# A graph layer whose row gathers are shared out: SyncE fetches one unit in 45 row by row, and the packing of edges is rewritten

## The chip, the core and the metric

The kernel runs on one core of one Trainium2 chip. A core has five engines, each with its own stream of instructions that it works off in order: PE (TensorE, matrix products), DVE (VectorE, elementwise work and sums), ACT (ScalarE), POOL (GpSimd) and SP (SyncE, which only issues transfers and waits). SP, ACT and POOL can issue DMA transfers; each has a queue of its own. The engines wait for each other by semaphores. SBUF is the on-chip memory of 128 partitions, PSUM the accumulator memory that PE writes, and DRAM holds inputs and outputs. The metric is the time of one execution on the device in microseconds (us), less is better.

## The reference

A message-passing layer on a graph with 50,000 nodes of 160 numbers and 1,650,000 edges, sorted by destination node (`dst`), followed by a residual and a layer norm. 50,000 of the edges are self loops (source = destination).

```python
s, v = x[:, :64], x[:, 64:].reshape(n, 32, 3)
ss, vv = s[src], v[src]                      # one row of x for each edge
e0, e1 = sh[:, 0:1], sh[:, 1:4]              # four numbers of each edge
dot = einsum('eui,ei->eu', vv, e1)
out0 = C0 * (ss * e0 @ W1 + dot * INV3 @ W2)
p3 = (ss @ W3)[:, :, None] * e1[:, None, :] * INV3
p4 = einsum('eui,uw->ewi', vv * e0[:, :, None], W4) * INV3
p5 = einsum('eui,uw->ewi', cross(vv, e1[:, None, :]), W5) * INV6
m = concatenate([out0, (C1 * (p3 + p4 + p5)).reshape(-1, 96)], axis=1)
m_agg = segment_sum(m, dst, num_segments=n)  # sum over the edges of each node
h = concatenate([m_agg[:, :64] @ Ws * LIN_S,
                 einsum('nui,uw->nwi', m_agg[:, 64:].reshape(n, 32, 3), Wv) * LIN_V ...])
return layernorm(x + (x + relu(h)))
```

What is computed is linear in `x[src]` for each of the four edge numbers, so the sums over edges can be taken before the weights.

## The kernel before

**Units, groups, pairs.** A unit is 128 edges, a group is 6 units (768 edges), a pair is two groups (12 units); 2100 groups make 12,600 units and 1050 pairs. The destinations of one group lie in a window of W = 32 nodes. For each unit POOL issues one indirect transfer (`gather`, L288), which fetches the 128 rows of x named by `si` into `xg`. DVE builds `hot` (L297: edge against slot in the window) and `ha` (L300: times the four edge numbers), and PE multiplies `ha` by the fetched rows into `ps` (L325), six units to a group. DVE or ACT takes `ps` to `A` (L334, L330). Four groups form a chunk: PE transposes it (L436), ACT copies it out (`at`, L439), PE applies the weights (L450), ACT copies the result to `hp` (L454). For each block of 128 nodes PE gathers the chunks that touch it (L480), and DVE and ACT add the residual and normalise (L176 to L192).

**Packing.** Self loops need no fetch from afar: their rows lie one after the other from the window's first node. Groups 100 to 2079 are made of L = 787 edges each, of which K = 19 self loops are taken out, so that 768 remain. `pack` does this for 120 groups at once, one to a partition, as a generator whose pieces are emitted between the pairs. It loads the edges (L351 to L354), casts them (L356), marks self loops (L370) and counts them (L371), then sums each of the four edge numbers of the self loops for each of the 32 slots (L389: one instruction for each of two halves of the row, four numbers and 32 slots, 256 in all), and closes the gaps with masked shifts (L406 to L416). The result goes to DRAM (`sd`, `ad`, L422, L423) and comes back with `load` (L241, L242). `own` fetches the 32 rows of each group's window, four copies, into `xo` (L315, the address comes from a register that L310 loads), and L334 adds `xo` times the self loops' sums (`taken`) to the group's sum.

**Order.** The work is emitted pair by pair in the loop of L595, with `own` three pairs ahead; a scheduler then orders each engine's stream and inserts the semaphore waits. SP issues nearly all transfers that are not gathers, ACT only the weights and the stores of the result (L192). The pools set how far an engine can be ahead: `rows` has six buffers of 12 units for `xg`, `own` four for `xo`, `psA` two for `ps`.

**Helpers, not in use.** The code already has a way to fetch a unit row by row with an ordinary queue (`fetch`, L505): 32 row offsets at a time are loaded into registers, and each row is one transfer. The table that says which engine does so, and every how many units, is empty:

```python
HELP = {}
...
for h, (eng, period) in enumerate(HELP.items()):
```

Of the kernel before, what the change touches and what calls it, by code (L numbers as in the profile page):

```python
# [34 lines left out]
F32 = mybir.dt.float32  # L35
# [9 lines left out]
P = 128  # L45
MUL0, MUL1 = 64, 32
D = MUL0 + 3 * MUL1
NK = 4
# [14 lines left out]
HELP = {}  # L63
HEAD = 100
RP = 120
ROWS = 32
# [28 lines left out]
def tile_gnn_resnorm(ctx: ExitStack, tc: tile.TileContext, x, src, dst, attr, W1, W2, W3, W4, W5, Ws, Wv, out, n_edges):  # L95
# [92 lines left out]
    def norm3(pool, y, mv, rstd, n, row):  # L188
        nc.vector.reciprocal(rstd[:n], rstd[:n])  # L189
        o = pool.tile([P, D], F32, name="o")  # L190
        nc.vector.tensor_scalar(o[:n], y[:n], mv[:n, 0:1], rstd[:n], op0=ALU.subtract, op1=ALU.mult)  # L191
        nc.scalar.dma_start(out[row, :], o[:n])  # L192
# [18 lines left out]
    with tc.tile_pool(name="once", bufs=1) as once, tc.tile_pool(name="raw", bufs=2) as rawp, \  # L211
            tc.tile_pool(name="idx", bufs=2) as idxp, tc.tile_pool(name="rows", bufs=6) as rowp, \
            tc.tile_pool(name="far", bufs=3) as farp, tc.tile_pool(name="own", bufs=4) as ownp, \
# [13 lines left out]

        offsets = {}
        evict = nc.vector.tensor_copy if ET.Activation in HELP else nc.scalar.copy

        def load(s):
# [4 lines left out]
            if NH <= g0 < NH + NPK:  # L236
# [3 lines left out]
                for i in range(2):  # L240
                    nc.sync.dma_start(rf[:n, i, :], sd[i:i + 1, e].rearrange("o (u p) -> (o u) p", p=P))  # L241
                nc.sync.dma_start(ra[:n].rearrange("u p k -> u (p k)"), ad[e].rearrange("(u p) k -> u (p k)", p=P))  # L242
# [3 lines left out]
            nc.sync.dma_start(ri[:n, 0, :], src1[e].rearrange("(u p) o -> u (p o)", p=P))  # L246
            nc.sync.dma_start(ri[:n, 1, :], dst1[e].rearrange("(u p) o -> u (p o)", p=P))
            nc.sync.dma_start(ra[:n].rearrange("u p k -> u (p k)"), attr[e].rearrange("(u p) k -> u (p k)", p=P))
# [55 lines left out]

        def own(p):

            s, g, ng = pairs[p]
            if not NH <= g < NH + NPK:
                return
            _, at = nc.values_load_multi_w_load_instructions(  # L310
                baseO[0:1, g:g + ng], engines=[ET.SP], min_val=0, max_val=(N - W) * 4 * D,
                skip_runtime_bounds_check_because="an offset of a row of x")
            xo = ownp.tile([P, PG, D], F32, name="xo")
            for i, v in enumerate(at):
                nc.sync.dma_start(xo[:, i, :].bitcast(U8),  # L315
                                  xbytes[ds(v, W * 4 * D)].rearrange("(w f) -> w f", w=W).unsqueeze(0)
                                  .to_broadcast([NK, W, 4 * D]))
# [20 lines left out]
        owns, stored, taken = {}, {}, {}  # L338
        halves = ((0, L // 2), (L // 2, L))

        def pack(c):
# [9 lines left out]
            nc.sync.dma_start(pri[:n, 0, :], src1[e].rearrange("(r e) o -> r (e o)", e=L))  # L351
            nc.sync.dma_start(pri[:n, 1, :], dst1[e].rearrange("(r e) o -> r (e o)", e=L))
# [468 lines left out]
```

## Time and profile before

| what | us |
|---|---|
| median of three runs | 18,925.2 (18,899.5 to 18,944.2) |
| the profiled execution | 15,879.8 |
| its span | 15,878.0 |
| busy: PE / POOL / DVE / ACT | 11,902 / 11,926 / 7,961 / 898 |
| transfers: bytes moved | 1382 MB, 87 GB/s |
| granted PE clock | 0.648 of full |

The profile is of one execution, and that one was shorter than the timed runs by a factor of 1.19. Busy time does not count the issuing of transfers by SP and ACT, nor the time between two instructions. The page cuts the span into 40 slices; the digits are tenths of busy time:

```profile
DVE  4565555545454554545454554545455454545422
...
POOL 7677777777777777777777777777777777777776
```

In groups of instructions, the columns are line, engine, operation, tiles and count, then the busy time in us and the mean of one in ns, then the engine's idle time ahead of the group and what ended it:

```profile
L389 DVE SCALAR_TENSOR_TENSOR waste<-marks,pra 120x393 bf16<-120x393 f32 (+3 forms) x4352 | 3652.5, 839 | 2.9
```

### The profile page before, as it was taken

To read this page: it belongs to the slowest core of one execution; us is meant where nothing else is said; L and a number is where in the kernel's file an instruction comes from. 1 tells how busy PE (TensorE), PEld (TensorE's weight loads), DVE (VectorE), ACT (ScalarE), POOL (GpSimd) and SP (SyncE) were. 2 spreads that over 40 slices of the span, in tenths; PEclk is the share of its full clock that TensorE was granted. 3 is DMA by queue.
4 is the path that set the end of the run, shared out by engine and by line. 5 is a ranking of instruction groups with operands and counts; after the bars stand their busy time and mean duration, and the time that the engine had idled before them with its cause. 6 is when DMAs were issued, how large, how long until landed. Compare 5 with 4: busy or idle time off the path is not lost. (4 is left out here: it accounts for less than half of the span.)

```text
span 15878.0 us, 132047 instructions
## 1 busy us (share of the span) xinstructions
PE 11902.0 (75%) x43059; PEld 8781.1 (55%) x43060; DVE 7960.7 (50%) x17460; ACT 897.9 (6%) x2069; POOL 11926.1 (75%) x12611
## 2 busy tenths in 40 slices
PE   7677777777777777777777777777777777777777
PEld 4455555555555555555555555555555555555555
DVE  4565555545454554545454554545455454545422
ACT  0000000000000000000000000000000000000000
POOL 7677777777777777777777777777777777777776
PEclk7666666666666666666666666666666666666666
DMA  3333333333333333333333333333333333333332
GB/s 83 74 86 94 84 82 96 82 95 84 94 83 92 85 82 96 83 96 83 94 85 87 91 82 96 84 94 84 94 83 82 96 82 96 83 93 84 86 83 70
DMA packets 1040422, 1382.05 MB, mean 87 GB/s; under 512 B 233153, under 2 KB 813393, under 8 KB 1035641
## 3 DMA queue, kind: packets, MB, share of 16 engines
q0 software_dynamic: 604800, 1033.00, 26.9%
q1 hardware_dynamic: 378065, 307.98, 7.1%
q10 hardware_dynamic: 56864, 32.58, 0.7%
q8 instruction: 344, 5.64, 0.1%
q14 instruction: 349, 2.86, 0.1%
HBM read 1303.90 MB, written 68.75 MB: 86 GB/s over the span
## 5 line engine op out<-in xcount | busy, mean ns | idle before, releaser
L288 POOL DMA_INDIRECT xg<-in_x,si x12600 | 11924.5, 946 | 3917.0 <-issue 3527.0
L325 PE MATMUL ps<-xg,ha 128*128 128x160 f32 x25200 | 8037.7, 447 | 3686.5 <-DMA xg<-in_x,si 3640.6
L325 PEld LDWEIGHTS ps<-xg,ha 128*128 128x128 f32 x25200 | 5302.5, 266 | 6227.7 <-DMA xg<-in_x,si 6033.2
L334 DVE SCALAR_TENSOR_TENSOR A<-xo,taken,ps 128x160 f32<-128x160 f32 x1980 | 728.8, 377 | 7231.3 <-PE ps L325 7231.3
L389 DVE SCALAR_TENSOR_TENSOR waste<-marks,pra 120x393 bf16<-120x393 f32 (+3 forms) x4352 | 3652.5, 839 | 2.9
L300 DVE TENSOR_TENSOR ha<-hot,pk 128x1536 f32<-128x1536 f32 x1050 | 1830.2, 1744 | 284.1 <-PE ps L325 284.0
L480 PE MATMUL phb<-hp,hot 128*128 128x160 f32 x4544 | 1181.0, 433 | 56.2 <-ACT at L439 52.8
L480 PEld LDWEIGHTS phb<-hp,hot 128*128 128x128 f32 x4544 | 1066.4, 297 | 173.3 <-ACT at L439 172.2
L436 PE MATMUL pt<-ident,A 128*128 128x128 f32 (+1 forms) x4200 | 1051.7, 406 | 100.1 <-ACT hp L454 67.8
L450 PE MATMUL phc<-BWb,at 32*128 32x160 f32 x4200 | 1078.0, 404 | 0.0
L439 ACT COPY at<-pt 128x512 f32<-128x512 f32 (+1 forms) x1050 | 596.9, 579 | 6815.1 <-PE pt L436 6746.4
L450 PEld LDWEIGHTS phc<-BWb,at 32*128 32x128 f32 x4200 | 835.0, 253 | 196.3 <-issue 196.1
L450 PE MATMUL phc<-BWa,at 128*128 128x160 f32 x4200 | 922.6, 374 | 2.3 <-ACT at L439 2.0
L436 PEld LDWEIGHTS pt<-ident,A 128*128 128x128 f32 (+1 forms) x4200 | 700.7, 178 | 302.7 <-ACT hp L454 143.1
L450 PEld LDWEIGHTS phc<-BWa,at 128*128 128x128 f32 x4200 | 847.0, 255 | 35.3 <-ACT at L439 35.3
L297 DVE TENSOR_TENSOR hot<-bank,rel 128x384 f32<-128x384 f32 x1050 | 569.6, 544 | 0.3
L454 ACT COPY hp<-phc 128x160 f32<-128x160 f32 x525 | 153.3, 292 | 6230.2 <-PE phc L450 6171.5
L470 DVE TENSOR_TENSOR hot<-bank,rr 128x768 f32<-128x768 f32 (+2 forms) x391 | 358.8, 918 | 0.1
L389 DVE DVE_READ_ACCUMULATOR waste<-marks,pra 120x1 f32 (+1 forms) x4352 | 342.9, 79 | 0.0
L416 DVE COPY_PREDICATED pra<-marks,pra 120x1572 f32<-120x1572 int32 (+6 forms) x170 | 323.5, 1903 | 0.0
L176 DVE SCALAR_TENSOR_TENSOR y<-phb,xt 128x160 f32<-128x160 f32 x391 | 120.6, 308 | 195.6 <-PE phb L480 195.3
L414 DVE COPY_PREDICATED prs<-marks,prs 120x393 f32<-120x393 int32 (+6 forms) x340 | 181.3, 582 | 0.1
(98 smaller groups left out, 1610.1 us busy)
## 6 DMA issues: line engine op xcount, KB each, us to landing
xg<-in_x,si POOLq DMA_INDIRECT x12600
xo<-in_x SPq DMA_DIRECT2D x1980, 80.0 KB
xt<-in_x SPq DMA_DIRECT2D x390, 80.0 KB
out<-o ACTq DMA_DIRECT2D x390, 80.0 KB
ra<-ad SPq DMA_DIRECT2D x99, 240.0 KB
pra<-in_attr SPq DMA_DIRECT2D x16, 1475.6 KB
ad<-pra SPq DMA_DIRECT2D x16, 1440.0 KB
rf<-sd SPq DMA_DIRECT2D x198, 60.0 KB
```

Of the source, the lines that this page charges most:

```text
L288: nc.gpsimd.indirect_dma_start(out=xg[:, j, :], out_offset=None, in_=x, in_offset=bass.IndirectOffsetOnAxis(ap=placed[0][:, u + j:u + j + ...
L297: nc.vector.tensor_tensor(hot[:, :n], slotsP[:, 0:W].unsqueeze(1).to_broadcast([P, n, W]), rel[:, u:u + n].unsqueeze(2).to_broadcast([P, n ...
L300: nc.vector.tensor_tensor(ha[:, :n], hot[:, :n].unsqueeze(2).to_broadcast([P, n, NK, W]), pk[:, :, u:u + n].rearrange("p k u -> p u k").un ...
L325: nc.tensor.matmul(ps[:, j // G, :], ha[:, j].rearrange("p k w -> p (k w)"), xr, start=j % G == 0, stop=j % G == G - 1)
L334: nc.vector.scalar_tensor_tensor(A[:, i], xo[:, i], taken[r // RP][:, r % RP:r % RP + 1], ps[:, i], op0=ALU.mult, op1=ALU.add)
L389: nc.vector.scalar_tensor_tensor(waste[:n, a:e], m[:, q], float(w + 1), pra[:n, a:e, k], op0=ALU.is_equal, op1=ALU.mult, accum_out=mine[:n ...
L416: nc.vector.copy_predicated(pra[:n, a:e], mi[:, r].unsqueeze(2).to_broadcast([n, e - a, NK]), pra[:n, a + d:e + d])
L436: nc.tensor.transpose(pt[:f1 - f0, g, :], A[:, i, f0:f1], ident)
L439: evict(at[:, :, :ng].rearrange("f k g w -> f g k w"), pt[:f1 - f0, :ng].rearrange("f g (k w) -> f g k w", w=W))
L450: nc.tensor.matmul(ph[:ng * W], at[:, k, :ng].rearrange("f g w -> f (g w)"), bw[:, k, :], start=i == 0, stop=i == 2 * NK - 1)
L470: nc.vector.tensor_tensor(hot2[:, :len(cs)], slotsP.unsqueeze(1).to_broadcast([P, len(cs), P]), rr[:, :len(cs)].unsqueeze(2).to_broadcast( ...
L480: nc.tensor.matmul(ph[:nb], hot2[:r, i, :nb], hp[:r], start=i == 0, stop=i == len(cs) - 1)
```

## The change

- `HELP` now names SP with a period of 45: of every 45 units the last of some pair is fetched by SP, 128 transfers of one row of 640 bytes, in four batches of 32 offsets (`ROWS`). POOL has 279 gathers less, 12,321. The offsets come from a copy of the source indices times 640 that ACT makes for each 20 groups (`ro`).
- All other transfers that SP issued go through ACT's queue (`dq`), `own` among them; it loads the addresses of ten groups at once (`OWN`), and `xo` has five buffers instead of four.
- The store of the result is issued one pair after its computation (`do_send`).
- In `pack` the sums for slot w run only over the part of the row where edges of that slot can lie (`early`, `late`), with two more limits that are tested at the end beside the others. That makes 168 instructions of 213 elements on average instead of 256 of 393.
- In `pack` the comparison of source and destination takes the destinations from a copy in PSUM, made by ACT; the count is capped in the scan itself, and operations from SBUF to SBUF are folded into others that have one operand in PSUM.
- Pauses (`yield`) stand between the loads and the cast of a pack, and ahead of its stores.

```diff
-HELP = {}
+HELP = {ET.SP: 45}
 HEAD = 100
 RP = 120
-ROWS = 32
+
+ROWS = {ET.SP: 32, ET.Activation: 16}
...
-                    nc.sync.dma_start(rf[:n, i, :], sd[i:i + 1, e].rearrange("o (u p) -> (o u) p", p=P))
-                nc.sync.dma_start(ra[:n].rearrange("u p k -> u (p k)"), ad[e].rearrange("(u p) k -> u (p k)", p=P))
+                    dq.dma_start(rf[:n, i, :], sd[i:i + 1, e].rearrange("o (u p) -> (o u) p", p=P))
+                dq.dma_start(ra[:n].rearrange("u p k -> u (p k)"), ad[e].rearrange("(u p) k -> u (p k)", p=P))
...
+        OWN = 5
+
         def own(p):
 
             s, g, ng = pairs[p]
             if not NH <= g < NH + NPK:
                 return
-            _, at = nc.values_load_multi_w_load_instructions(
-                baseO[0:1, g:g + ng], engines=[ET.SP], min_val=0, max_val=(N - W) * 4 * D,
-                skip_runtime_bounds_check_because="an offset of a row of x")
+            if p % OWN == 0:
+                g1 = min(g + OWN * PG, NH + NPK)
+                _, at = nc.values_load_multi_w_load_instructions(
+                    baseO[0:1, g:g1], engines=[ET.Activation], min_val=0, max_val=(N - W) * 4 * D,
+                    skip_runtime_bounds_check_because="an offset of a row of x")
+                places.update(enumerate(at, g))
             xo = ownp.tile([P, PG, D], F32, name="xo")
-            for i, v in enumerate(at):
-                nc.sync.dma_start(xo[:, i, :].bitcast(U8),
-                                  xbytes[ds(v, W * 4 * D)].rearrange("(w f) -> w f", w=W).unsqueeze(0)
-                                  .to_broadcast([NK, W, 4 * D]))
+            for i in range(ng):
+                dq.dma_start(xo[:, i, :].bitcast(U8),
+                             xbytes[ds(places.pop(g + i), W * 4 * D)].rearrange("(w f) -> w f", w=W).unsqueeze(0)
+                             .to_broadcast([NK, W, 4 * D]))
             owns[p] = xo
...
+        degree = n_edges / N
+        late = 6 * math.sqrt(L) + 2 * degree
+        early = -6 * math.sqrt(L)
...
+            for _ in range(3):
+                yield
             nc.scalar.copy(prs[:n], pri[:n])
             yield
             marks = psP.tile([P, 512], F32, name="marks")
             m, mi = marks[:n], marks[:n].bitcast(I32)
-            cum = packp.tile([P, L], F32, name="cum")
+
+            cum = packp.tile([P, L + 1], F32, name="cum")
             far = packp.tile([P, L], I32, name="far")
             less = packp.tile([P, L], I32, name="less")
-            carry = packp.tile([P, 1], F32, name="carry")
-            pbf = packp.tile([P, 1], F32, name="pbf")
+            pbf = packp.tile([P, 2], F32, name="pbf")
             mine = packp.tile([P, 2, NK * W], F32, name="mine")
             waste = packp.tile([P, L], BF16, name="waste")
-            nc.vector.tensor_scalar(pbf[:n], pb[:n], float(N - W), None, op0=ALU.min)
+            nc.vector.tensor_scalar(pbf[:n, 0:1], pb[:n], float(N - W), None, op0=ALU.min)
+            nc.vector.tensor_scalar(pbf[:n, 1:2], pbf[:n, 0:1], -1.0, None, op0=ALU.add)
+            nc.vector.memset(mine, 0.0)
+            nc.vector.memset(cum[:, 0:1], 0.0)
+
             for h, (a, e) in enumerate(halves):
                 q = slice(0, e - a)
-                nc.vector.tensor_tensor(m[:, q], prs[:n, 0, a:e], prs[:n, 1, a:e], op=ALU.is_equal)
-                nc.vector.tensor_tensor_scan(cum[:n, a:e], m[:, q], zeros[:n].to_broadcast([n, e - a]),
-                                             carry[:n] if h else 0.0, op0=ALU.add, op1=ALU.add)
-                nc.vector.tensor_copy(carry[:n], cum[:n, e - 1:e])
+                col = slice(2 * c + h, 2 * c + h + 1)
+                nc.scalar.copy(m[:, q], prs[:n, 1, a:e])
+                nc.vector.tensor_tensor(m[:, q], prs[:n, 0, a:e], m[:, q], op=ALU.is_equal)
+                nc.vector.tensor_tensor_scan(cum[:n, a + 1:e + 1], m[:, q], most[:n].to_broadcast([n, e - a]),
+                                             cum[:n, a:a + 1], op0=ALU.add, op1=ALU.min)
                 yield
 
-                nc.vector.scalar_tensor_tensor(m[:, q], cum[:n, a:e], float(K), m[:, q], op0=ALU.is_le, op1=ALU.mult)
-                nc.vector.tensor_scalar(cum[:n, a:e], cum[:n, a:e], float(K), None, op0=ALU.min)
-                nc.vector.scalar_tensor_tensor(far[:n, a:e], m[:, q], 0.0, cum[:n, a:e],
+                nc.vector.scalar_tensor_tensor(m[:, q], cum[:n, a:e], float(K), m[:, q], op0=ALU.is_lt, op1=ALU.mult)
+                nc.vector.scalar_tensor_tensor(far[:n, a:e], m[:, q], 0.0, cum[:n, a + 1:e + 1],
                                                op0=ALU.is_equal, op1=ALU.mult)
+
+                nc.vector.scalar_tensor_tensor(m[:, q], prs[:n, 1, a:e], pbf[:n, 1:2], m[:, q],
+                                               op0=ALU.subtract, op1=ALU.mult)
                 yield
-                nc.vector.tensor_scalar(cum[:n, a:e], prs[:n, 1, a:e], pbf[:n], None, op0=ALU.subtract)
-                nc.vector.tensor_reduce(packed[:n, 0, 2 * c + h:2 * c + h + 1], cum[:n, a:e], axis=AX.X, op=ALU.min)
-                nc.vector.tensor_reduce(packed[:n, 1, 2 * c + h:2 * c + h + 1], cum[:n, a:e], axis=AX.X, op=ALU.max)
-
-                nc.vector.scalar_tensor_tensor(m[:, q], cum[:n, a:e], 1.0, m[:, q], op0=ALU.add, op1=ALU.mult)
+                nc.vector.tensor_reduce(packed[:n, 0, col], prs[:n, 1, a:e], axis=AX.X, op=ALU.min)
+                nc.vector.tensor_reduce(packed[:n, 1, col], prs[:n, 1, a:e], axis=AX.X, op=ALU.max)
+                nc.vector.tensor_scalar(packed[:n, 0:2, col].rearrange("p a o -> p (a o)"),
+                                        packed[:n, 0:2, col].rearrange("p a o -> p (a o)"),
+                                        pbf[:n, 0:1], None, op0=ALU.subtract)
                 yield
-                for k in range(NK):
-                    for w in range(W):
-                        nc.vector.scalar_tensor_tensor(waste[:n, a:e], m[:, q], float(w + 1), pra[:n, a:e, k],
+
+                nc.vector.scalar_tensor_tensor(cum[:n, a:e], m[:, q], -degree, place_[:n, a:e], op0=ALU.mult, op1=ALU.add)
+                nc.vector.scalar_tensor_tensor(cum[:n, a:e], m[:, q], 0.0, cum[:n, a:e], op0=ALU.is_gt, op1=ALU.mult)
+                nc.vector.tensor_reduce(packed[:n, 2, col], cum[:n, a:e], axis=AX.X, op=ALU.min)
+                nc.vector.tensor_reduce(packed[:n, 3, col], cum[:n, a:e], axis=AX.X, op=ALU.max)
+                yield
+                for w in range(W):
+                    w0 = max(a, math.floor(degree * w + early))
+                    w1 = min(e, math.ceil(degree * w + late) + 1)
+                    for k in range(NK if w0 < w1 else 0):
+                        nc.vector.scalar_tensor_tensor(waste[:n, w0:w1], m[:, w0 - a:w1 - a], float(w + 1), pra[:n, w0:w1, k],
                                                        op0=ALU.is_equal, op1=ALU.mult,
                                                        accum_out=mine[:n, h, k * W + w:k * W + w + 1])
-                        if w % 4 == 3:
-                            yield
-            nc.vector.tensor_copy(counts[:n, c:c + 1], carry[:n])
+                    if w0 < w1:
+                        yield
+            nc.vector.tensor_copy(counts[:n, c:c + 1], cum[:n, L:L + 1])
...
-                        nc.vector.tensor_scalar(less[:n, a:e + d], far[:n, a:e + d], 0x7fffffff - d, None,
-                                                op0=ALU.bitwise_and)
+                        nc.vector.tensor_tensor(less[:n, a:e + d], far[:n, a:e + d], mi[:, 0:e + d - a],
+                                                op=ALU.subtract)
...
+            nbatch = P // ROWS[eng]
...
+                nr = ROWS[eng]
                 _, at = nc.values_load_multi_w_load_instructions(
-                    offsets[s][u:u + 1, i * ROWS:(i + 1) * ROWS], engines=[eng], min_val=0, max_val=(N - 1) * 4 * D,
+                    offsets[s][u:u + 1, i * nr:(i + 1) * nr], engines=[eng], min_val=0, max_val=(N - 1) * 4 * D,
                     skip_runtime_bounds_check_because="an offset of a row of x")
                 for j, v in enumerate(at):
-                    r = i * ROWS + j
+                    r = i * nr + j
                     queues[eng].dma_start(xr[r:r + 1, :].bitcast(U8),
                                           xbytes[ds(v, 4 * D)].rearrange("(o f) -> o f", o=1))
...
+        def do_send(b):
+            nb, row = rows_of(b)
+            dq.dma_start(out[row, :], outs.pop(b)[:nb])
...
+                    after_pair(p + 7, do_send, b)
```

In the rest of the diff `nc.sync` becomes `dq` in the same way, constants are set up (`most`, `place_`), and the count of pieces of `pack` is adjusted.

## The prediction

> **What bounds the kernel now.** I read the page's busy times first, then the table of stages, then GpSimd's waits. PE and GpSimd show 75% each, which decides nothing; the spacing of GpSimd's instructions does.
>
> ```profile
> PE 11902.0 (75%) x43059; PEld 8781.1 (55%) x43060; DVE 7960.7 (50%) x17460; ACT 897.9 (6%) x2069; POOL 11926.1 (75%) x12611
> ...
> L288 POOL DMA_INDIRECT xg<-in_x,si x12600 | 11924.5, 946 | 3917.0 <-issue 3527.0
> ```
>
> ```profile
> 14800.00:15200.00 400.00, 303.06 (x1086) 224.94 (x1086) 161.68 (x314) 21.68 (x51) 302.69 (x320) 0.64 0.34 87
> 15200.00:15600.00 400.00, 296.31 (x1092) 220.61 (x1092) 99.68 (x186) 23.07 (x52) 302.55 (x320) 0.67 0.33 82
> ```
>
> The last bracket before the clock is GpSimd: 320 gathers in 400 us, one every 1.25 us (946 ns and 0.30 us of issue). In the second stage the packing is over and VectorE has fallen from 162 to 100 us, yet the count is still 320. So GpSimd's own pace bounds, not VectorE, and 12,600 gathers x 1.25 = 15,750 of 15,878 us. GpSimd's waits say the same: "issue" is 3527 us, everything else is small.
>
> ```profile
> POOL xg L288 <- issue: 3527.0, 11578, 0.3
> POOL xg L288 <- DMA xg<-in_x,si: 149.3, 367, 3.0
> POOL xg L288 <- DVE si L273: 41.8, 2, 36.4
> ```
>
> PE is a follower: 3641 us of its waits on L325 end with the landing of xg.
>
> SP's queue, which the change turns over to row fetches, by line (minimum/median/maximum in ns):
>
> ```profile
> L315 SPq MOVE xo<-in_x x1980: 29/38/38, 46.9 to 15637.6; - x198
> L315 SPq DMA_DIRECT2D xo<-in_x x1980: 547/585/708, 47.0 to 15637.7; - x198
> ```
>
> ```profile
> L310 SPq TENSOR_LOAD <-baseO x990: 640/975/3587, 46.0 to 15623.3; - x198
> ```
>
> ```profile
> L423 SPq DMA_DIRECT2D ad<-pra x17: 314/317/504, 780.4 to 15040.2; - x17
> ```
>
> ```profile
> L192 ACTq DMA_DIRECT2D out<-o x391: 337/338/371, 167.4 to 15866.7; - x196
> ```
>
> A transfer whose address is in a register costs SP 38 + 585 ns; one with a fixed address can cost 314 to 338.
>
> [...]I therefore use the spacing, 1.25 us, not the 946 ns. [...]beside VectorE's SBUF-to-SBUF operations of L529 to L546 one gather takes 2.98 us, and beside L370, with two SBUF operands, 1.34. In the body it is not to be seen: the median is 946 and the minimum 940.
>
> ```profile
> 29.20 2.98 POOL L288 DMA_INDIRECT xg<-in_x,si  x1 [0.30 <-issue]
> 32.49 1.09 POOL L288 DMA_INDIRECT xg<-in_x,si  x1 [0.30 <-issue]
> 33.88 1.08 POOL L288 DMA_INDIRECT xg<-in_x,si  x1 [0.30 <-issue]
> 35.27 0.95 POOL L288 DMA_INDIRECT xg<-in_x,si  x1 [0.30 <-issue]
> 36.52 1.34 POOL L288 DMA_INDIRECT xg<-in_x,si  x1 [0.30 <-issue]
> ```
>
> [...]No run here shows a one-row transfer, so its issue is the unknown of this case.[...]
>
> **Time base.** The profiled execution took 15,879.8 us, the median of the runs 18,925.2: a factor of 1.192. [...]no trace shows a timed run, so it stays a guess. I sum in profiled time and multiply by 1.192, which assumes that GpSimd and SP slow down alike.
>
> **The change, part by part.**
>
> *Gathers.* 279 of 12,600 units leave GpSimd: 279 x 1.25 = 349 us less on the path. Behind them come the other gathers, 44.2 to a helped unit.
>
> *SP.* In their place stand 279 x 128 = 35,712 one-row transfers and 1116 register loads of 32 offsets. SP must do 128 rows while GpSimd does 44.2 gathers: 44.2 x 1.25 / 128 = 0.431 us a row. The cost of a row is one MOVE (38), its share of a load (975 / 32 = 30 if the load of 32 costs what the load of two does, about 60 at double) and the issue. Issue from below: 314, the shortest of any here; [...]I exclude much less, since 338 is so constant on ACT that most of it looks fixed. From above: 585, the xo issue, whose address is also in a register. The row lies between 0.38 and 0.68. I take 0.42: xo moves 128 rows in a three-dimensional broadcast, and I charge most of its 250 ns over L423 to that. This choice decides the case, as 35,712 x 0.442 + 100 already equals the old 15,880. At 0.42 SP needs 15.1 ms and stays hidden behind GpSimd; with that cover gone every 10 ns a row cost 357 us.
>
> *Order and waits.* In the built order every transfer of SP and ACT waits for the one eight places before it, whichever queue holds that: 2803 rows wait for a transfer of ACT, 2796 of ACT's 3208 for a row. So the queues run in step, and ACT's evictions stand behind its transfers. Following the semaphores through a middle stretch: gather 4296 needs the last row of unit 94, and row 40 of that unit needs gather 4225. Between lie 71 gathers, 89 us, against 88 rows, 37 us at 0.42; the tightest place I found leaves some 40 us for landings. This costs nothing while rows keep the pace. xg's six buffers (72 units, 90 us) stand between a stuck ACT and GpSimd.
>
> *ACT's queue* takes 1980 xo at 0.62, 198 loads of offsets (up to 10 values each) at about 1 us, 829 others at 0.4 and 391 stores at 0.34: 1.23 + 0.2 + 0.33 + 0.13 = 1.9 ms, plus its 0.9 ms of copies: 18% of the span. The waits of SP move there as well: 8763 us of L315 for VectorE's A. With five xo buffers for four, a load waits one pair (15 us) less, so I take most of it as gone; what stays delays an eviction that PE can spare. Two casts of half a row block per pack add 34 x about 0.5 us. The store of o goes one pair later, worth nothing. At the start the base_d transfers (6.25 us of issue) come ahead of the first cast: +6 us, never more, as it happens once.
>
> *Packing.* The sums fall from 256 per pack over 393 elements to 168 over 213 on average (with L = 787 and 33 edges to a node). [...]VectorE loses 1.9 to 2.4 ms off the path: worth 0, as the stage without packing showed. The operand in PSUM and the dropped SBUF-to-SBUF operations could give GpSimd at most what it lost, 15,878 - 15,750 = 128 us with start and end, and most of that is start, end and one stall. I take 0. The extra checks are four short operations per half.
>
> *The one stall.* At 800 us GpSimd waits 36.4 us for si, since the first pack is stored only at 778. In the new order that store needs gather 130, before 552. So the stall goes; but the pack's 150 to 180 us and eleven pairs of 4.3 us on VectorE must fit into the first 190 us, and up to 40 us of lag stand before xg's 90. I take 20 of the 36.
>
> Sum: 15,880 - 349 - 20 + 6 = 15,517; x 1.192 = 18,495 us.
>
> **Rivals.** *A, GpSimd's bound, fewer gathers (0.66):* 18,495, own range 18,420 to 18,620. For it: the unshaken 320 per stage; against it: the thin margin of 11 ns a row.
>
> *B, SP becomes the bound (0.23), slower.* Place: SP's row issue; price: 35,712 rows; it decides from 0.442 us. At 0.47 the profiled time is 16,885, the timed one 20,120; at xo's full 0.65 it is 27,800. For it: xo's 585 ns and the register address that rows share with it.[...]
>
> *C, between the two (0.05):* 0.432 to 0.442 a row, 18,500 to 18,925; I take 18,800.
>
> *D, the queues in step (0.06):* ACT stands behind rows, xg fills, GpSimd stalls once per helped unit. From 1.25 us a unit, 279 x 1.25 = 349, the gain is gone; at 1.5 us 18,580, at 3 us 19,080. Against it: the 40 us of room.
>
> The change's text about sums and PSUM as the real gain would be A with up to 60 us more (18,420), its lower end.
>
> **How the numbers follow.** No change is within 0.2%, 38 us, about what the runs' 45 us spread can tell. Faster: A, most of C and a share of D: 0.66 + 0.03 + 0.02 = 0.71. Same: 0.04. Slower: B and the rest of D, 0.25. The range starts at 18,420; upward it must take in C, D and the cheaper third of B, to 0.455 us a row: 16,350 x 1.192 = 19,490, leaving about 0.17 above and 0.03 below.
>
> **What would show it.** Right: GpSimd with 12,321 gathers still 1.25 us apart and waiting for "issue", SP's row issue with its MOVE and load under 431 ns and SP idle at times, PE's waits for xr small. Wrong: gathers spaced wider, waits of PE for xr and behind it of GpSimd for PE, SP without gaps (B); or SP with gaps that end on ACT's transfers (D).[...]

## The result: 1.55 times the time of the kernel before

| | us, median | runs |
|---|---|---|
| kernel before | 18,915.3 | 4 |
| changed kernel | 29,388.8 (29,344.0 to 29,420.5) | 4 |
| ratio | 1.5533, 95% interval 1.5504 to 1.5562 | |

The forecast was 18,495 us, its range ended at 19,490. The profiled execution of the changed kernel took 29,344 us, so its profile and the timed runs go together here.

One thing has to be known to read the numbers below. The experiments came in five series, each with the kernel before on the same chip. On one chip it took 18,925 us (first series) and 19,064 us (fifth); on three others 15,876, 15,877 and 15,872 us. The profile shown of before, 15,880 us, is like the three; the times of the result are like the one, which is called the first chip here. Every ratio stays within its own series.

**The profile after.** The page, first its busy times, then two groups of instructions (busy us, mean ns | idle us ahead of them and what ended it):

```profile
PE 8347.1 (28%) x43059; PEld 7276.5 (25%) x43060; DVE 6467.6 (22%) x14592; ACT 932.8 (3%) x2208; POOL 11651.5 (40%) x12333
...
L291 POOL DMA_INDIRECT xg<-in_x,si x12321 | 11649.2, 945 | 17557.8 <-PE ps L333 6676.7
...
L333 PE MATMUL ps<-xr,ha 128*128 128x160 f32 x558 | 244.3, 541 | 14683.1 <-DMA xr<-in_x 14683.1
```

GpSimd still takes 945 ns for a gather, but it idles 17.6 ms instead of 3.9. Every one of the 279 fetched units (558 = two passes each) is waited for: PE stands 14.7 ms for `xr`, 53 us a unit. GpSimd's waits (us in total, times, longest):

```profile
POOL xg L291 <- PE ps L333: 6676.7, 353, 84.9
POOL xg L291 <- PE pt L467: 6542.0, 140, 85.3
POOL xg L291 <- issue: 3550.9, 11642, 1.8
```

"issue" is what it was (3527 us). The two lines above it have grown from 196 and 0.3 us: PE stands before a fetched unit, frees no `xg`, and GpSimd stops. The same two stages as before, with GpSimd's busy time and count in the fifth bracket:

```profile
14800.00:15200.00 400.00, 119.03 (x624) 105.88 (x624) 57.18 (x106) 13.19 (x32) 166.39 (x176) 0.61 0.19 47
15200.00:15600.00 400.00, 122.56 (x637) 106.21 (x638) 61.41 (x114) 12.40 (x30) 167.02 (x177) 0.61 0.20 48
```

176 gathers in 400 us instead of 320. No engine is busy half of the time: this is a loss by waiting. What SP does, by line (minimum/median/maximum ns):

```profile
L547 SPq MOVE xr<-in_x x35712: 1/29/1680, 9.7 to 29319.1; - x200
L547 SPq DMA_DIRECT2D xr<-in_x x35712: 1/208/1954, 18.5 to 29319.2; - x200
```

A row costs 208 ns of issue and 29 of MOVE; undisturbed rows start 303 ns apart (median of all spacings). That is less than the 0.42 us forecast, so the price of a row isn't what failed.

### The profile page after: what moved, and what is told of

Its sections match the earlier page's. It is cut to its first block, busy times and chain, and to the rows that moved or that the text cites. A ratio compares the mean times of both kernels' runs of the same rounds, so it can differ in the third digit from the quotient of the medians.

```text
span 29342.1 us, 200447 instructions
## 1 busy us (share of the span) xinstructions
PE 8347.1 (28%) x43059; PEld 7276.5 (25%) x43060; DVE 6467.6 (22%) x14592; ACT 932.8 (3%) x2208; POOL 11651.5 (40%) x12333
## 5 line engine op out<-in xcount | busy, mean ns | idle before, releaser
L291 POOL DMA_INDIRECT xg<-in_x,si x12321 | 11649.2, 945 | 17557.8 <-PE ps L333 6676.7
L333 PE MATMUL ps<-xg,ha 128*128 128x160 f32 x24642 | 5236.3, 359 | 4017.2 <-issue 3798.4
L333 PEld LDWEIGHTS ps<-xg,ha 128*128 128x128 f32 x24642 | 4568.8, 236 | 4510.4 <-issue 4250.8
L333 PE MATMUL ps<-xr,ha 128*128 128x160 f32 x558 | 244.3, 541 | 14683.1 <-DMA xr<-in_x 14683.1
L418 DVE SCALAR_TENSOR_TENSOR waste<-marks,pra 120x236 bf16<-120x236 f32 (+45 forms) x2856 | 1498.9, 525 | 116.7 <-remote 12.5
L511 PE MATMUL phb<-hp,hot 128*128 128x160 f32 x4544 | 793.2, 325 | 285.8 <-issue 260.4
L511 PEld LDWEIGHTS phb<-hp,hot 128*128 128x128 f32 x4544 | 733.1, 212 | 309.9 <-issue 280.6
L481 PE MATMUL phc<-BWa,at 128*128 128x160 f32 x4200 | 719.7, 315 | 84.7 <-issue 84.0
L481 PE MATMUL phc<-BWb,at 32*128 32x160 f32 x4200 | 739.5, 316 | 5.1 <-issue 5.1
L481 PEld LDWEIGHTS phc<-BWb,at 32*128 32x128 f32 x4200 | 608.5, 192 | 103.8 <-issue 103.5
```

Source lines behind the costliest of these rows:

```text
L291: nc.gpsimd.indirect_dma_start(out=xg[:, j, :], out_offset=None, in_=x, in_offset=bass.IndirectOffsetOnAxis(ap=placed[0][:, u + j:u + j + ...
L333: nc.tensor.matmul(ps[:, j // G, :], ha[:, j].rearrange("p k w -> p (k w)"), xr, start=j % G == 0, stop=j % G == G - 1)
L418: nc.vector.scalar_tensor_tensor(waste[:n, w0:w1], m[:, w0 - a:w1 - a], float(w + 1), pra[:n, w0:w1, k], op0=ALU.is_equal, op1=ALU.mult, a ...
L481: nc.tensor.matmul(ph[:ng * W], at[:, k, :ng].rearrange("f g w -> f (g w)"), bw[:, k, :], start=i == 0, stop=i == 2 * NK - 1)
L511: nc.tensor.matmul(ph[:nb], hot2[:r, i, :nb], hp[:r], start=i == 0, stop=i == len(cs) - 1)
```

## The experiments

### First series (first chip): which part, and how much per unit

**The kernel before again**, no edit.

> The kernel before, unchanged, profiled once more, because its profile (15,880 us) and its timed runs (18,915 us) disagree while those of the changed kernel agree (29,342 and 29,389 us). If the first profile is typical, this one is 15,880 +- 50 us with gathers 1.25 us apart, and the timed runs differ by something a profile doesn't show. If the first profile was an exception, this one is 18,900 us and its trace shows which gathers are later than 1.25 us.

Measured: 18,928.3 us, ratio 0.9999 [0.9990, 1.0009], now with a profile of an execution as long as the timed ones (18,929 us). GpSimd's waits there:

```profile
POOL xg L288 <- issue: 3661.9, 11933, 2.1
POOL xg L288 <- PE ps L325: 1440.3, 239, 13.1
POOL xg L288 <- remote: 1011.3, 272, 7.1
POOL xg L288 <- DVE si L273: 491.4, 86, 107.3
```

"issue" has grown by 4%, not by a factor of 1.19, as it would if every engine ran slower; waits for PE and for what the profile can't name ("remote") have been added, 3 ms in all. So on this chip even the kernel before isn't bound by GpSimd alone.

**The change without its row fetches.**

```diff
-HELP = {ET.SP: 45}
+HELP = {}
```

> The changed kernel with an empty table of helpers: GpSimd gathers all 12,600 units, ACT still issues all other transfers, and the packing is the new one. Theory (the row fetches of SP and the transfers of ACT wait for each other in a circle that runs through PE's use of the fetched unit): without the rows the circle is gone, so the time is that of the kernel before within 1%, 18,700 to 18,950 us. Rival (ACT is what is overloaded, its evictions stand behind its transfers): still well above, over 21,000 us.

Measured: 18,925.8 us, ratio 1.0002 [0.9988, 1.0016]. ScalarE's queue with all the other transfers, the shorter sums and the operand in PSUM cost nothing and bring nothing here. The whole loss comes with the rows.

**Rows fetched but not used**: GpSimd gathers all units, the sums take its copy, and SP's rows land in a tile that nothing reads.

```diff
-                          [fetched.pop((p, h)) for _, h in helped.get(p, [])])
+                          [])
+            for _, h in helped.get(p, []):
+                fetched.pop((p, h))
```

> The changed kernel with all its 35,712 row fetches, but GpSimd gathers those 279 units as well and PE uses GpSimd's copy, so that nothing waits for the rows' data; the queues still share their semaphores. Theory of the circle through PE: the circle is cut, SP issues a row in about 0.3 us and has time to spare, so the time falls to that of the kernel before, 18,600 to 19,300 us. Rival (SP cannot issue or land rows faster than the 0.82 us seen, 35,712 x 0.82 = 29,300): it stays at 28,000 to 30,000 us.

Measured: 31,499 us, ratio 1.664 [1.6545, 1.6736], though no sum waits for a row. Neither theory had it: it is far above the first and above the 28,000 to 30,000 us of the second. So the idea of a circle that closes only where PE uses the fetched unit falls. The overview of waits shows another way round:

```profile
POOL xg L291 <- DVE rel L279: 13027.4, 101, 185.0
PEld bank L271 <- DMA rf<-sd: 11205.7, 180, 165.7
...
ACT ro L262 <- SPq L542: 8816.8, 87, 145.6
```

Read from below: ACT can't write the next `ro` (the offsets) until SP has loaded the old one into registers; in ACT's queue the loads of `rf` stand behind it; without `rf` no `rel` and no gather. SP is late, and ACT's in-order queue hands the delay on.

**One unit in 90.**

```diff
-HELP = {ET.SP: 45}
+HELP = {ET.SP: 90}
```

> The changed kernel with one unit in 90 fetched by SP. Theory of the circle: some 105 us per helped unit is what the circle takes, and 90 units take GpSimd 111 us at 1.25 us, so the circle just fits: 18,500 to 19,800 us. Rival (rows at 0.82 us each: half of them are 14,600 us): hidden behind GpSimd, 18,600 us. A time of 22,000 us or more speaks against both and for a cost of some 50 us per helped unit that is added to GpSimd's time.

Measured: 23,070 us, ratio 1.2187 [1.2149, 1.2226]: 30 us a unit for 139 units, against (29,389 - 18,915) / 279 = 37.5 in the changed kernel. Halving SP's rows did not open the lock on this chip.

### Second series: the rows alone, and what bounds the kernel before

From here on theory 1 is "order and waits": every transfer waits for the one eight places before it in one common order, so rows and ScalarE's transfers hold each other up. (The traces of the changed kernel bear the order out: the transfers of both engines end on the same eight semaphores, and 2803 rows come right behind a transfer of ScalarE on theirs.) Theory 2 is that rows are slow, or disturb, in themselves.

**All other transfers on GpSimd's queue.** SP's rows then share no order with other transfers.

```diff
-        dq = nc.scalar
+        dq = nc.gpsimd
...
-                    baseO[0:1, g:g1], engines=[ET.Activation], min_val=0, max_val=(N - W) * 4 * D,
+                    baseO[0:1, g:g1], engines=[ET.Pool], min_val=0, max_val=(N - W) * 4 * D,
```

> The changed kernel with all transfers that it sends through ScalarE's queue sent through GpSimd's queue instead; the 35,712 row fetches stay on SyncE as they are. So SyncE's rows no longer share completion semaphores and a common order with any other transfer. Theory 1 (rows and ScalarE's transfers hold each other up: each waits for the one eight places before it in one common order): the lock is gone, and what bounds is GpSimd, with 12,321 gathers and some 3,400 more issues at about 1.2 us each: 20,000 to 22,000 us, some 8 ms below the changed kernel although GpSimd does more. Theory 2 (128 one-row transfers and their register loads are slow in themselves, or slow others down): still 29,000 us or more.

**The same with `HELP = {}`.**

> The same with no row fetches: GpSimd issues all 12,600 gathers and all other transfers, SyncE nothing. It gives the base for the run before it. Both theories: 19,500 to 21,500 us. Theory 1: the rows add 0 to 1.5 ms to this when they are uncoupled (run before); theory 2: 9 ms or more.

Measured: 18,119.9 us with rows, 18,194.9 without; ratios to before 1.1415 [1.1396, 1.1434] and 1.1460 [1.1441, 1.1480]. Both lie below what was expected (from 20,000 and from 19,500 us). Uncoupled, the same 35,712 rows add nothing; they even bring 75 us, though less than the 279 gathers saved are worth (about 346 us at the 1.24 us of the run below). In the run with rows PE waits for them no more (group of instructions; last column):

```profile
L333 PE MATMUL ps<-xr,ha 128*128 128x160 f32 x558 | 169.0, 395 | 0.1
```

0.1 us, where the changed kernel shows 11,087 us on a chip of this kind (third series). Theory 2 falls for such a chip, with one reservation: GpSimd's queue now takes 18.2 ms even without rows, so that SP has 2.3 ms more for them than beside the kernel before.

**Fewer products**, and **fewer gathers**, in the kernel before:

```diff
             for j, xr in enumerate(rows):
+                if j % G == 2:
+                    continue
                 nc.tensor.matmul(ps[:, j // G, :], ha[:, j].rearrange("p k w -> p (k w)"), xr,
```

> The kernel before, with 2,100 of the 12,600 sum products on TensorE left out (one unit of every six is gathered but enters no sum, so its edges are missing from the output). If GpSimd bounds the timed executions, nothing changes: 18,900 us within 1%. If TensorE does (some 0.75 us a product, two passes of 373 ns in the profile of the repeated kernel before): 2,100 x 0.75 = 1.6 ms less, 17,300 us. Something between where GpSimd and TensorE take turns in waiting.

```diff
             for j in range(n - len(others)):
+                if j % G == 2:
+                    continue
                 nc.gpsimd.indirect_dma_start(
...
-            return [xg[:, j, :] for j in range(n - len(others))] + others
+            return [xg[:, j - (j % G == 2), :] for j in range(n - len(others))] + others
```

> The kernel before, with 2,100 of the 12,600 gathers left out (one unit in six enters the sums with the rows of its neighbour in its place, so the output has the wrong rows for those edges; all products are made). If GpSimd bounds the timed executions: 2,100 x 1.25 us = 2.6 ms less, 16,300 us. If TensorE does: 18,900 us within 1%. This is also the bound of what the change could ever gain: it takes away 279 gathers.

Measured: 15,859.8 us (0.9990 [0.9983, 0.9997]) and 13,267.4 us (0.8358 [0.8344, 0.8372]). 2100 gathers are worth 2608 us, 1.24 each; 2100 products nothing that matters. Where the kernel before takes 15,876 us GpSimd bounds it, as the forecast read from its profile.

### Third series: the order

**The changed kernel again**, on a chip where before takes 15,877 us.

> The changed kernel unchanged, beside the kernel before on this chip. The kernel before took 18,926 us in the first series and 15,876 us in the second, so the loss is wanted where GpSimd bounds it (15,876). Theory 1 (order and waits): the loss is a lock between queues, not a share of TensorE's time, so it stays in microseconds: between 24,500 and 29,400 us, 1.5 to 1.65 times the kernel before in either case.

Measured: 18,634.4 us, ratio 1.1725 [1.1706, 1.1744]: 2757 us more, 9.9 us a fetched unit, about a quarter of the loss on the first chip, and less than the expectation's 24,500. Its overview of waits, then GpSimd's and SP's:

```profile
PE ps L333 <- DMA xr<-in_x: 11086.8, 279, 77.9
```

```profile
POOL xg L291 <- PE ps L333: 1874.0, 256, 65.9
POOL xg L291 <- PE pt L467: 1335.0, 132, 48.9
```

```profile
SPq L547 <- DMA xo<-in_x: 3147.4, 1518, 59.1
```

GpSimd's two waits make 3209 us; less the 279 x 1.25 = 349 us of gathers saved, that is 2860, near the 2757 measured. And SP's rows wait above all for `xo`, a transfer of ScalarE. One turn of the lock from the timeline of this trace (start us, duration us, engine, line; in brackets the idle time ahead):

```profile
10073.38 1.11 PE L467 MATMUL pt<-ident,A 128*128 128x128 f32 x4 [32.13 <-DVE A L342]
...
10073.65 0.57 ACTq L323 DMA_DIRECT2D xo<-in_x  x1
...
10075.37 6.41 ACTq L323 DMA_DIRECT2D xo<-in_x  x4
...
10078.25 2.50 SPq L547 DMA_DIRECT2D xr<-in_x  x4
...
10080.12 0.94 POOL L291 DMA_INDIRECT xg<-in_x,si  x1 [60.60 <-PE ps L333]
```

Three rows of the next unit are out; the fourth stands behind `xo`, from 10,042 to 10,078, and ACT issues `xo` only when VectorE's `A` has freed the buffer. GpSimd stops for 60.6 us: for the first 21 PE waits for the rows of the unit before, which were late, then 32 for `A`, and GpSimd goes on when PE has made the sums behind it. And why was `A` late? The busy times of that stretch, in the order PE, PEld, DVE, ACT, POOL:

```profile
10042.00:10073.00 31.00, 0.00 (x0) 0.00 (x0) 29.15 (x106) 0.00 (x0) 0.00 (x0) 0.50 0.00 0
```

A good 100 instructions of the packing stand ahead of `A` in VectorE's queue. All others wait. So the circle is: sums behind rows, `A` behind sums (here behind packing too), `xo` behind `A`, the next rows behind `xo`.

**Rows first in the order.** Each transfer of ScalarE gets a dependency without a wait on the last row issued before it in the program, so that in the common order rows don't slip behind transfers of later pairs.

```diff
-        dq = nc.scalar
+        rows_at = [None]
+
+        class Behind:
+
+            def dma_start(self, *a, **k):
+                i = nc.scalar.dma_start(*a, **k)
+                if rows_at[0] is not None:
+                    tc.add_manual_dep(i.ins, rows_at[0].ins.name, mybir.DependencyInfo(
+                        mybir.DependencyClass.NoSync, mybir.DependencyReason.DATA), reason="behind the rows")
+                return i
+
+        dq = Behind()
...
-                    queues[eng].dma_start(xr[r:r + 1, :].bitcast(U8),
+                    rows_at[0] = queues[eng].dma_start(xr[r:r + 1, :].bitcast(U8),
```

> The changed kernel with one thing added: in the order in which transfers are dealt out to the semaphores, each transfer of ScalarE stands behind the rows of SyncE that the program issued before it (a dependency without a wait), so that rows no longer slip behind ScalarE's transfers of later pairs. Same work, same instructions. Theory 1 (rows slip back in the common order, and some 96 of a unit's 128 can only start after a transfer that needs TensorE): clearly faster than the changed kernel, by 2 to 5 ms. Theory 2 (the rows are slow or disturb in themselves): no change within 2%.

**Rows first, and a longer lead**: `q = at[-1] + 4` for `+ 2`, four buffers `far` for three.

> As the run before it, and each unit is fetched two pairs (24 units) earlier before its use, with four buffers for it in place of three. Theory 1: the rows of a unit now stand early enough in the order to start before the sums they used to wait for; another 1.5 to 3 ms less than the run before it. Theory 2: no change from the changed kernel.

**Longer lead only**: `q = at[-1] + 6`, five buffers, order as it was.

> The changed kernel with each unit fetched four pairs (48 units, more than one period of 45) earlier before its use, five buffers for it, nothing done to the order. Theory 1a (the rows' place in the common order decides): no gain, within 3% of the changed kernel, since the order is made as if SyncE were behind anyway and the rows slip back just as far. Theory 1b (a circle of one unit's length that has too little room): one more period of room, 57 us against the 48 us that a unit's rows and loads take, opens it, and the time falls to that of the kernel before or below. Theory 2: no change.

Measured: rows first 16,999.6 us (1.0695 [1.0677, 1.0713]), a gain of 1.6 ms where 2 to 5 were expected; with the longer lead 16,503.6 (1.0384 [1.0368, 1.0401]); the lead alone 18,646.3 (1.1733 [1.1714, 1.1752]), as if nothing had been done. The lead as such is worth nothing; the same rows in another order take back 1635 of 2757 us, and with the order right a longer lead takes back 496 more (less than the 1.5 to 3 ms expected). GpSimd's waits with both:

```profile
POOL xg L302 <- PE ps L344: 857.7, 247, 43.3
POOL xg L302 <- PE pt L478: 161.7, 52, 15.5
```

1019 us instead of 3209. Less the 349 us of gathers saved that is 670, near the 627 us by which this version is still slower than the kernel before.

### Fourth series: half the rows, the old queue, no rows

**One unit in 90, rows first**, with `+ 3` and four buffers; and **one unit in 90 again**, the first series' kernel.

> The changed kernel with one unit in 90 fetched, each transfer of ScalarE dealt out behind the rows issued before it, one pair more of lead and four buffers. If the lock is all that costs and it is open here, each of the 139 fetched units saves GpSimd a gather of 1.25 us: 15,877 - 174 = 15,700 us where GpSimd bounds the kernel before, the first version below it. If what remained in the run with rows first and longer lead (627 us for 279 units, 2.2 us a unit) is a price of the rows themselves: 15,877 + 139 x 2.2 = 16,190 us.

> The changed kernel with one unit in 90 fetched and nothing else altered (it ran in the first series at 1.2187 times the kernel before, 30 us a unit). By theory 1, where the kernel before takes 15,877 us, a unit costs up to the 9.9 us that it does in the changed kernel there, (18,634 - 15,877) / 279, less where rows have more slack: 15,900 to 17,250 us.

Measured: 15,685.1 us (0.9882 [0.9865, 0.9898]) and 15,671.5 us (0.9873 [0.9856, 0.9889]). Both are faster than the kernel before, the first as expected, the second against an expectation of 15,900 to 17,250 us; no order had to be set. PE's wait for rows in the second, then GpSimd's waits:

```profile
PE ps L333 <- DMA xr<-in_x: 4019.7, 137, 52.7
```

```profile
POOL xg L291 <- PE ps L333: 132.7, 434, 0.8
POOL xg L291 <- DMA xg<-in_x,si: 83.6, 148, 3.6
```

The rows are still late in 137 of 139 units, by up to 52.7 us. But GpSimd's longest wait for PE is 0.8 us: at half the rows the lock no longer reaches GpSimd on this chip. On the first chip this very kernel was 22% slower.

**Rows alone in the old queue**: the kernel before with `HELP = {ET.SP: 45}`.

> The kernel before with the row fetches alone (one unit in 45), all other transfers left in SyncE's queue and the packing as before. Rows then stand in one in-order queue with transfers that wait for TensorE. Theory 1: the lock is there with one queue too, 18,600 us or more (1.17 times the kernel before or worse), so moving the others to ScalarE's queue did not make it. If the common semaphores of two queues were the whole cause: at or below the kernel before.

Measured: 20,323.0 us (1.2806 [1.2785, 1.2828]), inside what theory 1 expected, but the trace doesn't show its lock. SP is at work in 17.1 of the 20.3 ms (rows, register loads and all other transfers, without gaps of over 0.3 us; in the changed kernel 13.5 of 18.6), which is more than the kernel before takes. And its rows wait for ScalarE's stores; for `xo` they wait 31 us in all.

```profile
SPq L515 <- DMA out<-o: 2832.3, 149, 180.4
```

So here SP's queue has too much work, and whether one queue would lock by order alone is not shown. The changed kernel, with the others on ScalarE's queue, takes 1.7 ms less; it has the shorter packing too, and the two parts were not tried apart.

**The rest of the change again**, `HELP = {}`.

> The changed kernel without row fetches, again: the rest of the change alone. In the first series it took 1.0002 times the kernel before. Where GpSimd bounds (15,876 us) it saves no gather: within 0.5% of the kernel before.

Measured: 15,837.4 us (0.9978 [0.9969, 0.9986]): 35 us less than before.

### Fifth series (the first chip again): is it TensorE that makes the lock dearer?

**Every sum product twice**, in the kernel before and in the changed kernel:

```diff
-            for j, xr in enumerate(rows):
+            for j, xr in list(enumerate(rows)) * 2:
```

> The kernel before with every sum product made twice on TensorE (the second pass starts the sum anew and overwrites the first): 12,600 products more, two passes of 136 ns each when they follow one another, 3.4 ms of TensorE's time. If GpSimd bounds it and TensorE has room: the kernel before within 0.5%, 15,870 us. If TensorE is near its bound: up to 3.4 ms more.

> The changed kernel with every sum product made twice. Theory 1: each fetched unit closes a circle rows - sums - ScalarE's transfer - rows, and TensorE's share of it, some 2 to 4 pairs of sums of 12 x 2 x 136 ns = 3.3 us more each, is paid once per unit: 279 x 6.5 to 13 us = 1.8 to 3.6 ms more than the changed kernel, 20,400 to 22,300 us, though TensorE stays idle most of the time and the same work costs the kernel before nothing. So a slower TensorE is multiplied by the lock, as in the first series. If the loss were fixed by SyncE's rows alone: 18,634 us within 1%.

Measured, beside 19,064 us for the kernel before: 19,389 us (1.0170 [1.0151, 1.0189]), between its two forecasts, and 28,185 us (1.4803 [1.4766, 1.4841]). A miss: the changed kernel did not take 1.8 to 3.6 ms more than its 29,389 us, but less (the kernel before took 18,915 us beside that, so the two can be set side by side). A longer share of TensorE in the circle isn't what makes it dear.

What the traces do show is where SP's time goes. Summed from its start times: in the third series rows less than 1 us apart take 10.8 ms, register loads 2.4, named waits 4.9, together 18.1 of 18.6 ms. SP is hardly ever idle without a named reason. That alone doesn't make it the bound: with one unit in 90 (fourth series) the same sums fill 15.0 of 15.7 ms, and GpSimd isn't held up. It counts here because PE waits for the rows of all 279 units, and GpSimd for PE. In the result's trace the sums are 10.0, 2.3 and 5.9, which leaves 11.1 ms; for most of that SP starts its instructions late and waits for nothing that the profile names. This rest, 0.5 against 11.1 ms, is about the difference between 18,634 and 29,389. A stretch from the timeline of the result's trace:

```profile
11175.81 0.43 PE L333 MATMUL ps<-xg,ha 128*128 128x160 f32 x1 [3.10 <-issue]
...
11176.51 0.29 PEld L333 LDWEIGHTS ps<-xg,ha 128*128 128x128 f32 x1 [1.82 <-issue]
11177.17 3.50 SPq L547 DMA_DIRECT2D xr<-in_x  x2
...
11177.91 0.43 PE L333 MATMUL ps<-xg,ha 128*128 128x160 f32 x1 [1.68 <-issue]
...
11179.31 0.29 PEld L333 LDWEIGHTS ps<-xg,ha 128*128 128x128 f32 x1 [2.51 <-issue]
```

PE's sums wait 1.7 to 3.1 us for "issue", that is for nothing that the profile shows, where TensorE's matmul records start 0.136 us apart in the median of this trace; two rows take SP 3.5 us instead of 0.6. What makes the starts late on this chip stays open.

## Why the prediction was wrong

- **Order and waits**, the step that failed. It saw that rows and ScalarE's transfers wait for each other, followed one path (gather, row, gather), found 40 us of room, put the term at nothing and said that this "costs nothing while rows keep the pace". Rows kept the pace (0.303 us), and net of the gather saved it cost 9.9 us a unit on one chip and 37.5 on the other. The path left out was the one from a row back to a row: row, sum, `A`, `xo`, next row. It asked how much room lies between two GpSimd instructions. The wait of `xo` for `A` it did see (8763 us); it took most of it as gone with a fifth buffer and let the rest delay only "an eviction that PE can spare". In the changed kernel's trace without rows (fourth series) about 3.7 ms of it are left, and in the common order it is the next rows that stand behind it. Shown by uncoupling (the rows add nothing) and by order alone (-1635 us), both on chips where GpSimd bounds the kernel before. On the first chip neither was tried: there it is shown that the whole loss comes with the rows, but not that this lock makes most of it.
- **Rival D** had the place right ("ACT stands behind rows, xg fills, GpSimd stalls once per helped unit") and "SP with gaps that end on ACT's transfers" as its sign. Its chance, 0.06, and its price, 1.25 to 3 us a unit, were the mis-sized terms. That price was meant before the gather's saving; GpSimd's two waits put it at 3209 / 279 = 11.5 us on the one chip and 13,219 / 279 = 47 on the first. Its sums were wrong as well: they take the saving off twice. 15,517 us already lacks the 279 gathers, so 1.5 us a unit makes 18,995 us and not 18,580, and 3 us makes 19,494, just past the end of the stated range, and not 19,080.
- **Packing, "off the path: worth 0"**, was right for the kernel before and wrong here. Once VectorE's `A` is in the circle, packing that stands ahead of it in VectorE's queue is on the path: 29 of 31 us in the stretch shown. That stretch is not typical: in the third series' trace GpSimd stands 2725 us in waits of over 5 us, and PE waits for `xr` in 1297 of them and for `A` in 516. How much of the loss goes when the packing does wasn't tried.
- **A row's price, "This choice decides the case"**: 0.42 us taken, 0.303 measured, with its share of a load (2.17 us for 32) 0.37. Under 0.442 either way. B's mechanism as priced didn't happen; but with 4.9 ms of waits on top of 13.2 ms of work SP's rows came late in every unit. The sum of B lacked the waits. The load was taken as 0.98 us, or double.
- **Time base**, the factor of 1.192. It was taken for one slowdown of GpSimd and SP alike, a guess by its own words. The runs contradict it: on the first chip gathers take 946 ns and "issue" 3662 us, 4% more than in the short execution, and the rest of the added time is waits. The factor is one of chips, and it was no factor for the change: before differs by 1.19, the changed kernel by 1.58.
- **Right**: GpSimd's bound where it takes 15.88 ms (1.24 us a gather). The saving of a gather, when no wait reaches GpSimd: 139 x 1.25 = 174 us and the 35 us of the rest make 209, measured 15,872 - 15,671 = 201. The rest of the change, forecast at -20 + 6 us, measured -35; GpSimd's wait for `si` fell from 41.8 to 15.0 us. The sums of the packing, forecast to cost VectorE 1.9 to 2.4 ms less (the author's estimate; the trace of before has no such sum over fewer elements than 393), cost 2.26 ms less: 3652.5 + 342.9 us with the accumulator reads before, 1499 + 235 us in the result's trace. ScalarE's queue carried its load at no cost.

With 35,712 rows of 0.3 us each, the time that it takes to issue transfers was not small here: SyncE was at work 17.1 ms with nearly all transfers in its queue and 13.5 ms with the others on ScalarE's (20,323 and 18,634 us, though the packing differs too). Moving them made the two queues wait for each other instead.

Two things stay open: what delays instruction starts on the first chip, and why GpSimd still waits 1019 us for PE with rows first and the longer lead. A version with one unit in 90 beats the kernel before by 1.2 to 1.3% on one chip and loses 22% to the kernel before on another, so it is no safe gain.

## What to carry to other kernels

When a helper queue is handed many small transfers, add up its work and then its waits: 13.2 ms of work looked safe under 15.9, and with 4.9 ms of waits its rows came late. A helper that is never idle proves nothing yet; look for who waits for it. Follow the semaphores from a transfer of the helper round to the helper's next one, through every in-order queue on the way, not only from the bottleneck to itself. And profile an execution that is as long as the timed ones before scaling anything: a span that differs by 1.19 may be another chip, not a slower clock.

## What the runs showed of the hardware

- One-row transfers from SyncE with the address in a register start 303 ns apart in the result's trace (MOVE 29 ns, issue 208), half of what a 128-row broadcast with its address in a register took to issue in the trace of before (585). A register load of 32 values took 2.17 us (third series), of two values 0.98 (before).
- VectorE's sums of the packing (L418, one operand in PSUM, in the result's trace, 120 partitions) took 161 ns at one element, 387 at 133 and 788 at 362, about 1.74 ns for each element more, and 82 ns more to read the accumulator.
- The first chip starts instructions of TensorE and SyncE late, in stretches of at least four at 0.65 to 5 us each, many of them near 0.7, 1.4 and 2.1 us apart. Such stretches hold 3.8 ms of TensorE's time in the kernel before (first series), and 5.6 of TensorE's and 4.6 of SyncE's in the result's trace; the changed kernel's trace from another chip (third series) has none on either engine, nor has the short execution of the kernel before. A lead and no more: in the result's trace 71% of TensorE's stretches and 55% of SyncE's begin within 20 us after a packet on the profile's "instruction" queue q8, where chance would give 23%; with the other one, q14, SyncE's show no such tie (50 against 53%). The mean granted clock does not tell the chips apart: 0.668 there in the kernel before, 0.648 in the short execution.
